# Order of the first steps of the last split in a graph-network kernel with residual normalisation

## Chip, cores and metric

One NeuronCore of a Trainium2 chip runs the whole program. The metric is the device time of one execution in microseconds (us). The engines are TensorE (PE in the profile, with PEld for its weight loads), VectorE (DVE), ScalarE (ACT), GpSimd (POOL) and SyncE (SP, which only issues transfers here).

## What is computed

The graph has 6250 nodes with 128 features and 100000 edges sorted by destination. Each edge gathers the features of its two ends and its own 128 attributes, multiplies the 384 values by W, normalises the 128 results, applies gamma, beta and relu, and its message is added to the node `src` of the edge. Each node's sum is added to its features and normalised again.

```python
msg_in = jnp.concatenate([x[row], x[col], edge_attr], axis=-1)
h = msg_in @ W + b
mu = jnp.mean(h, axis=-1, keepdims=True)
var = jnp.mean(jnp.square(h - mu), axis=-1, keepdims=True)
h = (h - mu) * jax.lax.rsqrt(var + LN_EPS) * gamma + beta
msg = jax.nn.relu(h)
out = jax.ops.segment_sum(msg, row, num_segments=x.shape[0])
...
x = _layernorm(x + out)
```

## The kernel before

The edges go through in six splits (`SPLITS`). The first half of the work on an edge computes the part of `h` that comes from the destination and the edge's own attributes, and scatters these rows to DRAM by an indirect transfer (L596), sorted by blocks of source nodes. The second half of the work loads the sorted rows back (`load_pair`, tile `hl`) and treats them by pairs of source blocks (`Pair`). Fifty blocks make 25 pairs per split; the last split has four tiles of 128 rows per pair. While the edges of one split are scattered, the pairs of the split before it are worked on (`FLOW`, `work`). After the last scatter has landed, nothing is left but the 25 pairs of the last split, and this tail is written out by hand: `head()` once and `tail(i)` for i = 0 to 24. The order of the calls is the order of the instructions on PE, DVE, ACT, SP and, in this part, POOL (`manual_schedule`).

One pair goes through these steps, which are called by these names below:

- **ones** (L668, DVE): the one-hot matrix `ohe` of the source node of each row, in one of four buffers.
- **turn** (L680, PE): four 128x128 transposes of `ohe` into a bank of PSUM, and **turned** (L684, ACT), the copy of that bank to `ohn` in SBUF, in one of two buffers.
- **seed**: the sorted rows are put into a PSUM bank (`sel` or `hp`). `seed_by_pe` (L696) does it with a product by the identity, in fp32; `seed` (L690) does it with a copy.
- **pick** (L710, PE): twelve bf16 products that add the source's features, held in three bf16 parts, to the seeded bank.
- **roots** (L1085 and L1089, ACT): four squares with sums, and the square root for the standard deviation.
- **scale** (L1145 and L735, DVE): the reciprocal, and four operations that give the messages `msg`, in one of two buffers.
- **sums** (L744, PE): four fp32 products of `ohe` and `msg`, which the profile counts as eight, into the one bank `pa`, and **add** (L762, DVE), which adds this bank to `acc`.
- For the blocks that are done, `Finish`: **load** (L774, SP) of the nodes' features `xs`, **begin** (L779 and L780, POOL), **stats** (L809, DVE), **squares** (L820, ACT) and **end** (L847, POOL). The last pair's blocks get theirs early, by `begin` and **counts** (L793, DVE).

PSUM has the banks `hp` (two), `sel` (three), `tr` (one), `pa` (one) and one for constants (`BANKS`, L35). In the tail before the change, all turns use `tr`, and pairs are seeded by PE into `sel` and `hp` in turn. Ahead of the tail PE runs some products on constants (`warm`, L1181); the last four of these wait for the last scatter. In `head()`, `work(1)` and `work(4)` are the last steps of the pair that is left over from the split before: its sums, then its add ("old sums" and "old add" below).

Of the kernel before, what the change touches and what calls it, by code (L numbers as in the profile page):

```python
# [8 lines left out]
F32 = mybir.dt.float32  # L9
BF16 = mybir.dt.bfloat16  # L10
# [6 lines left out]
P = 128  # L17
D = 128
# [9 lines left out]
PT = 4  # L28
# [6 lines left out]
BANKS = {"hp": 2, "sel": 3, "tr": 1}  # L35
# [31 lines left out]
def dram_ap(t, offset, ap):  # L67
    return bass.AP(tensor=t.tensor, offset=t.offset + offset, ap=ap)
# [12 lines left out]
def flat(t):  # L81
    return t.rearrange("p t d -> p (t d)")


def fast_path(ctx, tc, io, bad_d):
# [3 lines left out]
    nc = tc.nc  # L89
# [3 lines left out]
    psum = ctx.enter_context(tc.tile_pool(name="psum", bufs=1, space=bass.MemoryType.PSUM))  # L93
# [5 lines left out]
    def pe(i, cost=1):  # L99
        done.append((i.ins, cost))  # L100
        return i
# [69 lines left out]
    iota_p, zero_p, at = beside[:, 0:P], beside[:, P:P + 1], beside[:, P + 8:P + 8 + NB]  # L171
# [167 lines left out]
    acc = tabs.tile([P, NB, ACW], F32, name="acc")  # L339
# [306 lines left out]
    def load_pair(s, p):  # L646

        k = 2 * SPLITS[s][1]
        pair = late["blk"].tile([P, KMAX, ROW], F32, name="hl", bufs=4)
        nc.sync.dma_start(flat(pair[:, :k, :]),  # L650
                          dram_ap(sorted_d[s], p * k * P * ROW, [[k * ROW, P], [1, k * ROW]]))
        loaded[s, p] = pair

    class Pair:
# [14 lines left out]
                                    self.hl[:, :k, D:D + 1].to_broadcast([P, k, P]),  # L669
                                    row_bc(iota_p, k), op=ALU.is_equal)  # L670

        def turn(self):

            self.ohn = late["blk"].tile([P, KMAX, P], BF16, name="ohn", bufs=2)
            half = self.ohe.bitcast(BF16)
            for j0, m in [(0, self.k)]:
                tr = psum.tile([P, PT, P], F32, name="tr", bufs=BANKS["tr"]).bitcast(BF16)
                tr = tr.rearrange("p t (h d) -> p (t h) d", h=2)
                for j in range(m):
                    pe(nc.tensor.transpose(tr[:, j, :], half[:, j0 + j, 1::2], ident_h))  # L680
                self.tr = tr
# [1 line left out]
        def turned(self):  # L683
            nc.scalar.copy(self.ohn[:, :self.k, :], self.tr[:, :self.k, :])  # L684

        def seed(self, g):

            j0, m = self.groups[g]
            self.sel[g] = psum.tile([P, PT, P], F32, name="sel", bufs=BANKS["sel"])
            nc.scalar.copy(self.sel[g][:, :m, :], self.hl[:, j0:j0 + m, 0:D])  # L690

        def seed_by_pe(self, g):
            j0, m = self.groups[g]
# [182 lines left out]
    tr = psum.tile([P, PT, P], F32, name="tr", bufs=BANKS["tr"])  # L876
# [102 lines left out]
    def work(n):  # L979

        nonlocal n_steps
        for _ in range(n):
            for off, step in FLOW:
                i = n_steps - LEAD - off
                if i % 4 or not 0 <= i // 4 < len(pairs):
                    continue
                if step is None:
                    load_pair(*pairs[i // 4])
                    continue
                if off == 0:  # L990
                    at_work[i // 4] = Pair(*pairs[i // 4])
                step(at_work[i // 4])
            n_steps += 1
# [24 lines left out]
    for s, (n_tiles, _, _, _) in enumerate(SPLITS):  # L1018
        p0, p1 = first_tile[s] // PT, -(-first_tile[s + 1] // PT)
        slots = p1 - p0  # L1020
        for i in range(slots):
# [14 lines left out]
            n = steps_due(q + 1) - n_steps  # L1036
# [28 lines left out]
    s, n = n_split - 1, NB // 2  # L1065
    x = [Pair(s, p) for p in range(n)]
    f = [Finish(2 * p, 2) for p in range(n)]

    def at(p):
        return 0 <= p < n  # L1070
# [5 lines left out]
    def squares_of(i):  # L1076
        if i not in squares:
            squares[i] = late["blk"].tile([P, PT + FN], F32, name="ss6", bufs=4)
        return squares[i]

    def roots(i):
        ss = squares_of(i)
        sq = late["blk"].tile([P, PT, P], F32, name="sq")
        for j in range(PT):
            nc.scalar.activation(sq[:, j, :], x[i].sel[0][:, j, :], AF.Square, scale=float(D),  # L1085
                                 accum_out=ss[:, j:j + 1])
        c = PT + FN if at(i - 4) else PT
        std = late["blk"].tile([P, PT + FN], F32, name="std6", bufs=4)
        nc.scalar.activation(std[:, :c], ss[:, :c], AF.Sqrt, bias=eps, scale=1.0 / D ** 3)  # L1089
        x[i].std[0] = std  # L1090

    def head():
        for p in range(2):
            x[p].ones()
            load_pair(s, p + 2)
        x[0].seed_by_pe(0)
        x[0].turn()
        x[0].turned()
        f[0].load()
        work(1)  # L1100
        x[1].turn()
        x[1].turned()
        f[1].load()
        work(4)
        x[2].ones()
        load_pair(s, 4)

    both = {name: late["fin"].tile([P, 2 * FN], F32, name=name + "4", bufs=1)
            for name in ("total", "var", "std", "rstd", "shift")}
# [2 lines left out]

    def tail(i):
        x[i].pick(0)
        if i in (1, 2):
            x[i + 1].turn()
        roots(i)
        if i in (1, 2):
            x[i + 1].turned()
        if i and i + 1 < n - 1:  # L1120
            f[i + 1].load()
        if i == 0:
            f[n - 1].load()
        if i == 1:
            x[2].seed_by_pe(0)
        if at(i - 1):
            x[i - 1].sums()
        if i > 1 and at(i + 1):
            x[i + 1].seed_by_pe(0)
        if i > 1 and at(i + 2):  # L1130
            x[i + 2].turn()
        if at(i - 3) and at(i + 1):
            squares_of(i + 1)
            f[i - 3].squares(squares[i + 1][:, PT:])
        elif at(i - 3):
            f[i - 3].squares(both["var"][:, 0:FN])
        if i > 1 and at(i + 2):
            x[i + 2].turned()
        if i == n - 1:
            f[i - 2].stats()  # L1140
        if i >= n - 2:
            x[i - 1].add()
        c = PT + FN if at(i - 4) else PT
        rstd = late["blk"].tile([P, PT + FN], F32, name="rstd6", bufs=4)
        nc.vector.reciprocal(rstd[:, :c], x[i].std[0][:, :c])  # L1145
        x[i].rstd[0] = rstd
        if at(i - 4):
            f[i - 4].rstd = rstd[:, PT:]
        if 0 < i < n - 2:
            x[i - 1].add()  # L1150
        x[i].scale(0)
        if at(i + 5):
            load_pair(s, i + 5)
        if at(i - 1):
            f[i - 1].begin()
        if i == 1:
            f[n - 1].begin()
        if at(i - 2) and i < n - 1:
            f[i - 2].stats()
        if at(i - 4):  # L1160
            f[i - 4].moved()
            f[i - 4].end(nc.gpsimd, nc.sync)
        if i == 2:
            f[n - 1].counts(acc[:, 2 * n - 2:2 * n, D:D + 1])
        if at(i + 3):
            x[i + 3].ones()

    n_last = 4 * len(pairs) + LEAD + 14
# [27 lines left out]
    for i in range(n):  # L1196
        tail(i)
# [274 lines left out]
```

## Time and profile before

| quantity | value |
|---|---|
| runs shown | 1100.59, 1098.43 and 1100.34 us, median 1100.34 us |
| the profiled execution, its own time | 1102.5 us |
| its span, first to last instruction | 1100.6 us |
| mean granted clock of TensorE | 0.891 |
| busy shares | PE 78%, DVE 79%, ACT 67%, POOL 75% |
| last scatter issued | 1013.55 us, landed by 1015.62 us |
| first squares of the last split | 1023.06 us |
| last instruction that computes | 1094.4 us |

The tail that the change touches is the stretch from about 1015 us to the end. Rows of the timeline give start and length in us, engine, line, operation and tiles, the count, and in brackets the idle time of the engine ahead of it and what ended it. Rows of the chain give the start, the length and what the program's end was waiting for then. Rows by stretches give the stretch, its length, the busy time of PE with its count of products, the granted clock (1.00 is full speed), the busy share of the DMA engines and GB/s.

### The profile page before, as it was taken

The numbers are of one execution on the slowest core, as the hardware profiler recorded it, in microseconds if no ns is written. First come the engines' busy times: TensorE is split into PE (matmuls) and PEld (weight loads), VectorE is DVE, ScalarE is ACT, GpSimd is POOL, SyncE is SP. The second block draws the span as 40 slices with busy tenths as digits, with TensorE's granted clock in tenths as the row PEclk, the third lists the DMA queues.
The fourth block names the chain that finished last, engine by engine and source line by source line (L and its number), as shares of the span: only waits on it lengthen the run. The fifth ranks groups of instructions, "written<-read, shape, count | busy, mean of one in ns | idle before, by whom it ended". The sixth has DMA issues, their size and how long they took to land.

```text
span 1100.6 us, 27337 instructions
## 1 busy us (share of the span) xinstructions
PE 861.5 (78%) x8722; PEld 797.5 (72%) x8722; DVE 865.8 (79%) x2399; ACT 732.3 (67%) x3093; POOL 820.8 (75%) x907
## 2 busy tenths in 40 slices
PE   6757764638786968788877878888988899987996
PEld 4656764527776867787767778888988798885775
DVE  8875888336787877777787777988999998876897
ACT  3333331116666767576667677987989899986797
POOL 5777777777777777777777777777777777776586
PEclk8878786567898998888989898998999999999998
DMA  6999997367686865686777658876878677762563
GB/s 203 280 286 281 290 294 239 116 200 243 211 280 218 256 198 154 226 259 217 254 245 232 198 159 290 272 238 225 274 231 275 214 209 232 235 180 89 169 200 112
DMA packets 126451, 247.31 MB, mean 225 GB/s; under 512 B 47314, under 2 KB 60868, under 8 KB 126296
## 3 DMA queue, kind: packets, MB, share of 16 engines
q1 hardware_dynamic: 100118, 191.57, 57.7%
q0 software_dynamic: 25024, 52.85, 13.4%
q8 instruction: 70, 1.15, 0.5%
q10 hardware_dynamic: 1154, 1.05, 0.3%
q14 instruction: 85, 0.70, 0.2%
HBM read 155.48 MB, written 89.90 MB: 223 GB/s over the span
## 4 chain that ended last, share of the span: by engine, by line
PE 29%; DMA 28%; DVE 21%; ACT 13%; issue 5%; POOL 2%; SPq 1%; ACTq 0%; POOLq 0%; DVEq 0%
DMA sorted<-hs,place_i 20%; PE pa L744 8%; PE hp L555 7%; PE sel L710 6%; DVE msg L735 6%; DMA db<-drel_d 4%; DVE sc L412 4%; DVE ohe L668 3%; ACT sq L719 2%; POOL sorted L596 2%; PE beside L448 2%; ACT sel L690 2%; ACT sq L1085 2%; ACT ohn L684 2%; DMA eT<-in_eT 2%
## 5 line engine op out<-in xcount | busy, mean ns | idle before, releaser
L596 POOL DMA_INDIRECT sorted<-hs,place_i x782 | 760.3, 972 | 243.8 <-issue 106.0
L710 PE MATMUL sel<-xa,ohn 128*128 128x128 bf16 x2706 | 201.2, 226 | 99.2 <-ACT sel L690 98.3
L555 PE MATMUL hp<-w,eT 128*128 128x128 f32 x1564 | 244.0, 305 | 37.8 <-ACT hs L575 32.7
L575 ACT COPY hs<-hp 128x512 f32<-128x512 f32 x195 | 113.5, 582 | 240.0 <-DMA sorted<-hs,place_i 186.1
L744 PE MATMUL pa<-msg,ohe 128*128 128x130 f32 x1900 | 262.5, 290 | 11.5 <-DVE acc L762 8.2
L710 PEld LDWEIGHTS <-ohn 128*128 128x128 bf16 x2850 | 184.0, 101 | 111.6 <-issue 94.5
L735 DVE SCALAR_TENSOR_TENSOR msg<-sel,rstd,cut 128x128 f32<-128x128 f32 x902 | 255.3, 345 | 8.0
L744 PEld LDWEIGHTS pa<-msg,ohe 128*128 128x128 f32 x1900 | 238.9, 201 | 17.5 <-DVE acc L762 11.6
L555 PEld LDWEIGHTS hp<-w,eT 128*128 128x128 f32 x1564 | 218.0, 215 | 42.1 <-ACT hs L575 36.0
L719 ACT ACTIVATE sq<-sel 128x128 f32<-128x128 f32 x850 | 224.3, 282 | 17.5 <-PE sel L710 17.0
L719 ACT ACTIVATION_READ_ACCUMULATOR sq<-sel 128x1 f32 x850 | 180.4, 212 | 0.0
L668 DVE TENSOR_TENSOR ohe<-hl,beside 128x1024 f32<-128x1024 f32 (+2 forms) x150 | 148.6, 991 | 37.3 <-DMA hl<-sorted 31.5
L690 ACT COPY sel<-hl 128x512 f32<-128x512 f32 (+1 forms) x225 | 127.9, 568 | 16.3 <-DVE msg L735 16.1
L684 ACT COPY ohn<-tr 128x1024 bf16<-128x1024 bf16 (+2 forms) x150 | 123.3, 822 | 12.4 <-PE tr L680 12.2
L545 DVE TENSOR_SCALAR ohd<-db,part_w 128x512 bf16<-128x512 bf16 x192 | 70.6, 368 | 46.7 <-DMA db<-drel_d 29.8
L728 DVE RECIPROCAL rstd<-std 128x4 f32<-128x4 f32 (+1 forms) x225 | 38.5, 171 | 78.2 <-ACT std L722 77.5
L680 PE MATMUL tr<-ident_h,ohe 128*128 128x128 bf16 x950 | 81.4, 226 | 9.7 <-DVE ohe L668 9.6
L567 PE MATMUL hp<-win,ohd 126*128 126x128 bf16 x782 | 82.8, 232 | 1.3 <-DMA win<-xb_d 0.8
L680 PEld LDWEIGHTS <-ohe 128*128 128x128 bf16 x950 | 62.9, 101 | 26.1 <-DVE ohe L668 24.1
L722 ACT ACTIVATE std<-ss,eps 128x4 f32<-128x4 f32 (+1 forms) x225 | 66.9, 297 | 7.3
L567 PEld LDWEIGHTS <-ohd 126*128 126x128 bf16 x782 | 66.5, 105 | 5.8 <-DVE ohd L545 1.1
L762 DVE TENSOR_TENSOR acc<-acc,pa 128x260 f32<-128x260 f32 x124 | 51.1, 412 | 23.2 <-PE pa L744 22.4
(196 smaller groups left out, 838.4 us busy)
## 6 DMA issues: line engine op xcount, KB each, us to landing
eT<-in_eT SPq DMA_DIRECT2D x96, 512.0 KB
hl<-sorted SPq DMA_DIRECT2D x75, 528.0 KB
db<-drel_d SPq DMA_DIRECT2D x96, 256.0 KB
sorted<-empty SPq DMA_DIRECT2D x100, 198.0 KB
hl<-sorted SPq DMA_DIRECT2D x50, 264.0 KB
sorted<-hs,place_i POOLq DMA_INDIRECT x782
hl<-sorted SPq DMA_DIRECT2D x25, 396.0 KB
sorted<-empty SPq DMA_DIRECT2D x50, 132.0 KB
```

The lines of the kernel that those rows point to most:

```text
L555: pe(nc.tensor.matmul(hp[:, j, :], eT[:, at], w[:, 2, :], start=j == 0, stop=False, skip_group_check=True), 4)
L567: pe(nc.tensor.matmul(hp[:, j, :], oh[:3 * WN, at], win[:3 * WN, :], start=False, stop=j == m - 1, skip_group_check=True))
L575: nc.scalar.copy(hs[:, :m, 0:D], hp[:, :m, :])
L596: i = nc.gpsimd.indirect_dma_start(out=sorted_d[s][:, :], out_offset=bass.IndirectOffsetOnAxis(ap=place_i[:parts, t:t + 1], axis=0), in_=h ...
L668: nc.vector.tensor_tensor(self.ohe[:, :k, :], self.hl[:, :k, D:D + 1].to_broadcast([P, k, P]), row_bc(iota_p, k), op=ALU.is_equal)
L680: pe(nc.tensor.transpose(tr[:, j, :], half[:, j0 + j, 1::2], ident_h))
L684: nc.scalar.copy(self.ohn[:, :self.k, :], self.tr[:, :self.k, :])
L690: nc.scalar.copy(self.sel[g][:, :m, :], self.hl[:, j0:j0 + m, 0:D])
L710: pe(nc.tensor.matmul(sel[:, j, :], self.ohn[:, j0 + j, :], xa[:, b, i * D:(i + 1) * D], start=False, stop=j == m - 1 and i == 2, skip_gro ...
L719: nc.scalar.activation(sq[:, j, :], self.sel[g][:, j, :], AF.Square, accum_out=ss[:, j:j + 1])
L735: nc.vector.scalar_tensor_tensor(self.msg[:, j0 + j, 0:D], self.sel[g][:, j, :], rstd[:, j:j + 1], cut, op0=ALU.mult, op1=ALU.max)
L744: pe(nc.tensor.matmul(self.pa[:, h, :], self.ohe[:, j, :], self.msg[:, j, :], start=(j == h), stop=(j == k - 2 + h)), 4)
```

## The change

Only `head()`, the first four calls of `tail(i)` and two helpers change; all instructions up to the start of `head()` stand in the same order on PE. `turn` and `seed` take the name of a bank, and `seed` the engine of its copy:

```diff
-        def turn(self):
+        def turn(self, name="tr"):
...
-                tr = psum.tile([P, PT, P], F32, name="tr", bufs=BANKS["tr"]).bitcast(BF16)
+                tr = psum.tile([P, PT, P], F32, name=name, bufs=BANKS[name]).bitcast(BF16)
...
-        def seed(self, g):
+        def seed(self, g, copy=nc.scalar.copy, name="sel"):
...
-            self.sel[g] = psum.tile([P, PT, P], F32, name="sel", bufs=BANKS["sel"])
-            nc.scalar.copy(self.sel[g][:, :m, :], self.hl[:, j0:j0 + m, 0:D])
+            self.sel[g] = psum.tile([P, PT, P], F32, name=name, bufs=BANKS[name])
+            copy(self.sel[g][:, :m, :], self.hl[:, j0:j0 + m, 0:D])
```

```diff
         for p in range(2):
             x[p].ones()
             load_pair(s, p + 2)
+        f[n - 1].load()
+        work(1)
         x[0].seed_by_pe(0)
         x[0].turn()
         x[0].turned()
+        x[1].turn("hp")
+        x[1].turned()
+        x[1].seed(0, nc.vector.tensor_copy, "hp")
         f[0].load()
-        work(1)
-        x[1].turn()
-        x[1].turned()
         f[1].load()
-        work(4)
         x[2].ones()
         load_pair(s, 4)
+        work(4)
+        x[3].ones()
...
         x[i].pick(0)
-        if i in (1, 2):
-            x[i + 1].turn()
+        turns = {0: (2, "tr"), 1: (3, "sel"), 3: (4, "tr")}.get(i)
+        if turns:
+            x[turns[0]].turn(turns[1])
         roots(i)
-        if i in (1, 2):
-            x[i + 1].turned()
+        if turns:
+            x[turns[0]].turned()
         if i and i + 1 < n - 1:
             f[i + 1].load()
-        if i == 0:
-            f[n - 1].load()
-        if i == 1:
-            x[2].seed_by_pe(0)
-        if at(i - 1):
-            x[i - 1].sums()
-        if i > 1 and at(i + 1):
+        if i > 1:
+            x[i - 1 if i > 2 else 0].sums()
+        if i and at(i + 1):
             x[i + 1].seed_by_pe(0)
-        if i > 1 and at(i + 2):
+        if i == 2:
+            x[1].sums()
+        if i > 2 and at(i + 2):
             x[i + 2].turn()
...
+        if i == 2:
+            x[0].add()
+            f[0].begin()
+            x[4].ones()
...
-        if 0 < i < n - 2:
+        if 1 < i < n - 2:
             x[i - 1].add()
         x[i].scale(0)
...
-        if at(i - 1):
+        if i > 1:
             f[i - 1].begin()
-        if i == 1:
+        if i == 0:
             f[n - 1].begin()
+            f[n - 1].counts(acc[:, 2 * n - 2:2 * n, D:D + 1])
...
-        if i == 2:
-            f[n - 1].counts(acc[:, 2 * n - 2:2 * n, D:D + 1])
-        if at(i + 3):
+        if i > 1 and at(i + 3):
             x[i + 3].ones()
```

The rows below show how this moves the instructions at three places. First PE, at the start of `head()`, before the change (`pa` with `msg_2126` are the old sums; of the four transposes and their weight loads one is shown):

```order
L1192 TENSOR_LOAD bad_t
L696 MATMUL sel<-hl,ident 128x512
...
L680 MATMUL tr<-ident_h,ohe 128x128
L744 MATMUL pa<-msg_2126,ohe 128x130 x4
...
L710 MATMUL sel<-xa,ohn 128x128
...
L696 MATMUL hp<-hl,ident 128x512
...
```

And the same place with the change:

```order
L1197 TENSOR_LOAD bad_t
L744 MATMUL pa<-msg_2126,ohe 128x130 x4
L696 MATMUL sel<-hl,ident 128x512
...
L680 MATMUL tr<-ident_h,ohe 128x128
...
L680 MATMUL hp<-ident_h,ohe 128x128
...
L710 MATMUL sel<-xa,ohn 128x128
...
```

The old sums now stand ahead of the first seed, the turn of pair 1 follows that of pair 0 at once in another bank, and the seed of pair 1 (`hp<-hl`) is gone from PE.

Second ACT, from the start of `head()` on, before (the numbers at `ss` and `std` tell the pairs apart: `ss_15388` is pair 0, `ss_15428` pair 1, `ss_15481` pair 2, `ss_15537` pair 3):

```order
L684 COPY ohn<-tr 128x512 x2
L1085 ACTIVATE sq,ss_15388<-sel 128x128 x4
L1089 ACTIVATE std_15394<-ss_15388,eps 128x4
L1085 ACTIVATE sq,ss_15428<-hp 128x128 x4
L1089 ACTIVATE std_15434<-ss_15428,eps 128x4
L684 COPY ohn<-tr 128x512
L1085 ACTIVATE sq,ss_15481<-sel 128x128 x4
L1089 ACTIVATE std_15487<-ss_15481,eps 128x4
L684 COPY ohn<-tr 128x512 x2
L1085 ACTIVATE sq,ss_15537<-hp 128x128 x4
```

And with the change (pairs 0 to 3 are `ss_15400`, `ss_15440`, `ss_15473` and `ss_15536`):

```order
L684 COPY ohn<-hp 128x512
L1085 ACTIVATE sq,ss_15400<-sel 128x128 x4
L1089 ACTIVATE std_15406<-ss_15400,eps 128x4
L684 COPY ohn<-tr 128x512
L1085 ACTIVATE sq,ss_15440<-hp 128x128 x4
L1089 ACTIVATE std_15446<-ss_15440,eps 128x4
L684 COPY ohn<-sel 128x512
L1085 ACTIVATE sq,ss_15473<-sel 128x128 x4
L1089 ACTIVATE std_15479<-ss_15473,eps 128x4
L1085 ACTIVATE sq,ss_15536<-hp 128x128 x4
L1089 ACTIVATE std_15542<-ss_15536,eps 128x4
L684 COPY ohn<-tr 128x512
```

The copy for pair 2 now stands behind the root of pair 0 and that for pair 3 behind the root of pair 1, and the copy for pair 4 has moved behind the root of pair 3.

Third DVE, at the same place, as a piece of the difference (`msg_2127` is pair 0 and later pair 2, `msg_2126` pair 1):

```order
+L690 COPY hp<-hl 128x512
 L668 TENSOR_TENSOR ohe<-hl,beside 128x512
-L1145 RECIPROCAL rstd_15398<-std_15394 128x4
-L735 SCALAR_TENSOR_TENSOR msg_2127<-sel,rstd_15398,cut 128x128 x4
+L762 TENSOR_TENSOR acc<-acc,pa 128x260
 L668 TENSOR_TENSOR ohe<-hl,beside 128x512
-L1145 RECIPROCAL rstd_15446<-std_15434 128x4
-L762 TENSOR_TENSOR acc<-acc,pa 128x260
-L735 SCALAR_TENSOR_TENSOR msg_2126<-hp,rstd_15446,cut 128x128 x4
+L1151 RECIPROCAL rstd_15409<-std_15406 128x4
+L735 SCALAR_TENSOR_TENSOR msg_2127<-sel,rstd_15409,cut 128x128 x4
+L793 SCALAR_TENSOR_TENSOR last_y<-beside,acc,last_y 128x128 x2
```

DVE now copies the rows of pair 1 into `hp`, makes the one-hots of pairs 2 and 3 ahead of the first messages, and does the counts of the last blocks between the messages of pairs 0 and 1. On SP, the load of `xs` for the last blocks stands ahead of those for pairs 0 and 1, and the load of pair 5's rows follows that of pair 4's without one of `xs` in between; on POOL, `begin` of the last blocks stands ahead of that of pair 0.

More of the change, by code (lines that the diff above doesn't have):

```diff
@@ L1136, in tail @@
             f[i - 3].squares(both["var"][:, 0:FN])
-        if i > 1 and at(i + 2):
+        if i > 2 and at(i + 2):
             x[i + 2].turned()
```

## Prediction

> **What bounds the kernel now.** I read the chain of waits first, from the last scatter to the end, since only the tail changes.
>
> ```profile
> 1023.93 0.67 PE hp L710 x12
> 1024.60 0.22 PE tr L680 x4
> 1024.83 0.91 PE sel L696 x2
> ...
> 1030.57 0.95 PE pa L744 x8
> 1031.52 0.86 PE sel L696 x2
> ...
> 1033.37 1.15 ACT sq L1085 x8
> 1034.52 0.02 issue
> 1034.55 0.30 ACT std L1089
> 1034.85 0.77 ACT fsq L820 x4
> 1035.62 0.47 ACT ohn L684
> ...
> 1084.76 1.14 ACT sq L1085 x8
> ```
>
> From the landing of the first rows at 1018.39 to the squares of pair 4 at 1033.37 the chain lies on PE without a gap. From there ACT repeats squares, root, squares of the finished blocks and copy, 19 times in 1084.76 - 1033.37 = 51.39 us, or 2.70 a pair. The change leaves this steady part and the last steps as they are. So what it is worth is how much earlier the squares of pair 4 start: **1033.37** is the number to move. Second I read how PE begins, in the timeline.
>
> ```profile
> 1015.62 1.89 PE L1181 MATMUL tr<-ones_h 128*128 128x512 bf16 x4 [3.94 <-DMA sorted<-hs,place_i]
> 1018.39 2.07 PE L696 MATMUL sel<-hl,ident 128*128 128x512 f32 x2 [0.89 <-DMA hl<-sorted]
> 1020.26 0.63 PE L680 MATMUL tr<-ident_h,ohe 128*128 128x128 bf16 x4
> 1020.69 1.44 PE L744 MATMUL pa<-msg,ohe 128*128 128x130 f32 x8
> ...
> 1022.19 0.83 PE L710 MATMUL sel<-xa,ohn 128*128 128x128 bf16 x12
> ```
>
> PE stands still for 0.89 us between the products on constants and the first seed, and the seed takes 1020.26 - 1018.39 = 1.87 us, where later ones take 0.91. The granted clock says why, in stretches of 3.41 us that fit its steps:
>
> ```profile
> 106.59:110.01 3.42, 2.88 (x15) 0.50 0.93 269
> 110.01:113.42 3.41, 2.60 (x15) 0.50 0.96 338
> 669.79:673.20 3.41, 2.84 (x22) 0.50 1.04 391
> 673.20:676.61 3.41, 3.41 (x42) 1.00 1.03 358
> 1011.12:1014.53 3.41, 0.56 (x3) 1.00 0.18 60
> 1014.53:1017.94 3.41, 1.89 (x4) 0.50 0.33 91
> 1017.94:1021.36 3.42, 2.96 (x9) 0.50 0.91 298
> 1021.36:1024.77 3.41, 3.41 (x42) 1.00 0.39 127
> ```
>
> After the idle stretch from 1011.12 the clock is halved; it comes back at 1021.36, behind a stretch in which PE was busy for 2.96 us. Elsewhere 2.84 of 3.41 us busy was enough and 2.88 was not, so the border lies about there; 1.89 us did not do.
>
> **The change part by part**, first with the clock as it was here, full from 1021.36 on.
>
> *Old sums first.* They leave 1020.69 and start behind the products on constants, at 1015.62 + 1.89 = 1017.51. At full clock they take 0.95 us by the chain, so at half clock about 1.9: until 1019.4, past the landing of the rows by 1.0. The seed follows with its 1.87 to 1021.3, then the turn of pair 0 to about 1021.6, and its copy. In exchange nothing stands between the two turns any more:
>
> ```profile
> 1020.93 0.59 ACT L684 COPY ohn<-tr 128x512 bf16<-128x512 bf16 x1 [10.86 <-PE tr L680]
> ```
>
> The first copy starts at 1021.7 instead of 1020.93 and takes 0.59, so the first pick starts at 1022.3 where it was 1022.19: **0.1 us later**. The old pick had waited for the old sums and the second turn, not for its copy.
>
> *Seed of pair 1 on DVE.* PE loses one seed, **0.91 us** on the chain. DVE gains a copy of 128x512 from SBUF to PSUM, which the trace does not show. The nearest rows are ACT's copy of that size and DVE's of a quarter of it:
>
> ```profile
> 1004.88 0.58 ACT L690 COPY sel<-hl 128x512 f32<-128x512 f32 x1
> ...
> 1008.99 0.29 DVE L1186 COPY beside<-beta 128x128 f32<-128x128 f32 x1
> ```
>
> It costs between 0.29 and four times that, 1.16; I take 0.6. DVE has the two first one-hots behind it at 1019.8 and is next needed for the root of pair 0 at about 1024.6. In between lie this copy, two one-hots and the old add, by the rows further down 0.6 + 2 x 0.68 + 0.43 = 2.4 of the 4.8 us, so even 1.16 is hidden.
>
> *Turns sooner, one-hots sooner.* No turn is added; each only stands ahead of a pick or of sums where it stood behind one before, so that ACT's copy is done while PE is at other work.
>
> *Sums of pairs 0 and 1 put off to step 2.* Here new waits come in, so I walk through PE, starting with pick 0 at 1022.3 (pick 0.67, turn 0.22, seed 0.88 between the two rows of it, sums 0.95). Up to pick 2 stand two picks, two turns and a seed: 1024.95. Pick 2 needs the copy for pair 2, which ACT makes behind pair 0's squares and root: squares start 0.87 behind the pick (1022.19 and 1023.06 before), so 1023.2 + 1.16 + 0.30 + 0.5 = 1025.2: a wait of 0.25. The sums of pair 0 and the seed of pair 3 end at 1027.7. The sums of pair 1 now meet the one bank `pa`: they need the add of pair 0, which stands on DVE behind the messages of pair 1. These start at 1026.8 (copy to 1025.2, squares and root of pair 1 to 1026.65, reciprocal) and take, as do the other operations of DVE here, by the rows
>
> ```profile
> 1025.82 0.68 DVE L668 TENSOR_TENSOR ohe<-hl,beside 128x512 f32<-128x512 f32 x1
> 1026.41 0.17 DVE L1145 RECIPROCAL rstd<-std 128x4 f32<-128x4 f32 x1
> 1026.67 0.43 DVE L762 TENSOR_TENSOR acc<-acc,pa 128x260 f32<-128x260 f32 x1
> 1027.01 1.12 DVE L735 SCALAR_TENSOR_TENSOR msg<-hp,rstd,cut 128x128 f32<-128x128 f32 x4
> ```
>
> Messages and add are 1.12 + 0.43 with an overlap of 0.1: 1028.2, a wait of 0.5. Queued behind these sums are pick 3 and, through it, ACT's squares of pair 3. Pick 3 ends at 1029.8, its turn, the sums of pair 2, the seed of pair 4 follow, the turn of pair 5 waits some 0.1 for its one-hot on DVE, and pick 4 starts at 1032.2, where it was 0.87 ahead of 1033.37, or 1032.50.
>
> The **sum** in this clock: 0.1 later at pick 0; off PE go the seed's 0.91 and the waits that it had between pick 0 and pick 4, which are the 10.31 us between them less four picks, turns and seeds and three sums (9.93), or 0.38; new waits of 0.25 + 0.5 + 0.1 = 0.85 come in. That is **-0.3 us**: squares of pair 4 at 1033.1, and 1102.2 for the profiled execution's 1102.5 (its span is 1100.6). The unknown copy adds nothing between its bounds. The new waits, which I added up from rows, may come to between 0 and 1.5 us: -1.2 to +0.3.
>
> *The clock.* The steps of the granted clock lie on a grid of 3.41 us, and in this execution a boundary, 1017.94, lies just ahead of the first seed. Before the change, a stretch that holds the whole idle 0.89 has at most 2.52 us busy, less than the 2.88 that did not do, so a sufficient one begins at 1017.8 or later and full clock comes between 1021.2 and 1024.6, by where the grid lies: on average 1022.9. This execution had nearly the best case. With the old sums in the gap PE is busy from 1015.62 on; a sufficient stretch may begin at 1015.0, and full clock comes between 1018.4 and 1021.8, on average 1020.1. A product takes twice as long at half clock, so each us of it on PE's chain costs 0.5: (1022.9 - 1020.1) x 0.5 = **1.4 us** on average. That nothing fixes the grid to the program is my choice; one trace can't show it, though the runs shown, 2.16 us apart, leave room for it.
>
> The Trainium skill, "TensorE: Matmul & The Clock Gate", Part 1, says that the clock is released by a window of 4096 cycles (3413 ns) that runs freely and lies differently from run to run; the steps of 3.41 us agree, the free running no run here shows yet. The same part advises against fitting to the cold start, since it varies; by that alone the sum would be the 0.3 without the 1.4.
>
> Together 0.3 + 1.4: **-1.7 us** from the median of 1100.34, which is **1098.6**. In the profiled execution's own terms the change gives 1102.2 if the grid lies as it did, and at best, with full clock at 1018.4, half of 3.0 us less, 1100.7. The profiled time is 2.2 above the median, and I take the difference over to the median unchanged.
>
> **The rivals.**
>
> *Only the order counts* (the clock comes back where it did, as the grid goes with the program): -0.3, 1100.0. For it speaks that one grid is all I have seen; against it the spread of the runs.
>
> *The put-off sums cost nothing.* If DVE is quicker with the messages of pair 1 and the add, PE runs without the 0.85 of new waits; then -0.3 - 0.85 - 1.4, or 1097.8. ACT allows it: from pair 0's squares at 1023.2 it has four times squares and root (1.45), four copies (0.47) and 0.77 before pair 4, and so 1031.7. Against it speaks the single bank `pa`.
>
> *Slower: the counts hold DVE.* They now stand ahead of pair 1's messages and wait for POOL's `begin` of the last blocks, which needs the old add (about 1021.5) and the loaded `xs`. By the rows
>
> ```profile
> 1028.63 0.69 POOL L779 TENSOR_TENSOR last_y<-acc,g 128x256 f32<-128x256 f32 x1
> 1029.39 0.73 POOL L780 TENSOR_TENSOR last_y<-last_y,xs 128x256 f32<-128x256 f32 x1
> ```
>
> POOL's two operations end 1.49 us after they start, so they are ready by about 1023 to 1024, and the counts' turn comes at 1026. Each us that POOL ends after 1026 shifts pair 1's messages, its sums, pick 3 and the end by a us. For more than 2.2 us slower in all it would have to end at 1030. Against it speaks the transfer row: what was issued by 1021.3 had landed when the queue fell silent.
>
> ```profile
> 1023.00:1024.00 1.00, 1.00 (x8) 0.43 (x7) 0.18 (x1) 0.94 (x8) 0.00 (x0) 1.00 0.03 9
> ```
>
> Here the DMA share is 0.03. If it happened, 1103.
>
> **How the numbers follow.** Forecast 0.62 (1097.8 to 1099.4), only the order 0.18 (1099.3 to 1100.6), no new waits 0.13 (1096.8 to 1098.1), slower 0.07. A measurement of this kernel can tell about 0.2% or 2.2 us from no change, so faster means below 1098.1. That takes the third case and about a third of the first, 0.13 + 0.20 = 0.33; slower 0.05 of the last case; the rest is the same, 0.62. The range leaves out the slower case and the ends of the others: 1096.9 to 1100.5.
>
> **What would show it.** The old sums start at about 1017.5, with no idle between the constants and the seed. Full clock comes at 1021.8 or sooner after a landing at 1015.6; if later, the clock term is wrong. The sums of pair 1 wait some 0.5 for the add of pair 0; if not, the second rival. ACT's squares of pair 3 follow an idle of about 1 us, and those of pair 4 start 0.3 us sooner after the last landing (17.75 us before) if the clock comes as here, up to 1.8 sooner if it comes at the earliest. The prediction is wrong if the 2.70 a pair changes, or if counts wait.

## The result and the profile after

| | before | with the change |
|---|---|---|
| median of 22 runs each, the two kernels on one chip | 1100.46 us (1096.01 to 1104.4) | 1097.92 us (1095.55 to 1100.33) |
| ratio, 95% interval | | 0.9981, [0.9972, 0.999] |
| profiled execution, own time and span | 1102.5 and 1100.6 us | 1095.55 and 1094.0 us |
| first load of the last split's rows behind the last landing, issued | 1015.71 us | 1010.22 us |
| first squares of pair 4 | 1033.37 us | 1025.99 us |
| between these two | **17.66 us** | **15.77 us** |

The forecast was 1098.6 us, so 1.7 less; measured is 2.5 less by the medians and 2.1 by the ratio. The same change once more, in a later set of runs, gave 1099.35 us for 1099.32 and a ratio of 0.9999 [0.9986, 1.0013]. Both ratios weighted by the inverse squares of their half-widths give 0.9987, give or take 0.0008: 0.7 to 2.3 us faster. The two do not agree well, and the traces will say why executions differ so.

The spans of the two profiled executions differ by 6.6 us, but 5.49 us of that lie ahead of the tail: the last scatter was issued and landed that much earlier, where no instruction was moved on PE. So I compare the last row of the table, 1.89 us. Of this stretch, PE first (timeline of the change; start, length, engine, line, operation, count, idle time ahead):

```profile
1010.27 1.89 PE L1186 MATMUL tr<-ones_h 128*128 128x512 bf16 x8
1012.00 1.06 PE L744 MATMUL pa<-msg,ohe 128*128 128x130 f32 x8
1013.01 1.12 PE L696 MATMUL sel<-hl,ident 128*128 128x512 f32 x2
1013.97 0.39 PE L680 MATMUL tr<-ident_h,ohe 128*128 128x128 bf16 x4
1014.45 0.40 PE L680 MATMUL hp<-ident_h,ohe 128*128 128x128 bf16 x4
1015.03 0.84 PE L710 MATMUL sel<-xa,ohn 128*128 128x128 bf16 x12 [0.19 <-ACT ohn L684]
1016.25 0.40 PE L680 MATMUL tr<-ident_h,ohe 128*128 128x128 bf16 x4 [0.37 <-DVE ohe L668]
```

Constants, old sums and seed follow each other without idle time, where before there were 3.94 us of waiting for the scatter and 0.89 for the rows. That the first of these two is gone is chance (the scatter was early); that the second is gone is the change. The seed takes 1.12 us where it took 2.07: the clock was not halved at all. By stretches of 3.41 us that fit the steps of the clock in this execution (length, then busy time and count of PE, PEld, DVE, ACT, POOL, then granted clock, DMA share, GB/s):

```profile
1005.52:1008.93 3.41, 2.77 (x29) 1.97 (x26) 2.32 (x10) 2.40 (x16) 2.78 (x3) 1.00 0.18 60
1008.93:1012.34 3.41, 3.06 (x20) 2.20 (x21) 1.93 (x7) 0.73 (x5) 0.00 (x1) 1.00 0.32 84
1012.34:1015.76 3.42, 3.14 (x29) 2.02 (x27) 2.23 (x4) 1.07 (x2) 0.00 (x0) 1.00 0.92 317
```

On DVE and ACT of the same timeline stand the new copy, the counts, the add that frees `pa`, the put-off sums of pair 1, and the squares of pair 3:

```profile
1014.31 0.69 DVE L690 COPY hp<-hl 128x512 f32<-128x512 f32 x1
...
1018.75 0.60 DVE L793 SCALAR_TENSOR_TENSOR last_y<-beside,acc,last_y 128x128 f32<-128x128 f32 x2
...
1020.52 0.41 DVE L762 TENSOR_TENSOR acc<-acc,pa 128x260 f32<-128x260 f32 x1
...
1020.99 1.16 PE L744 MATMUL pa<-msg,ohe 128*128 128x130 f32 x8
...
1022.86 0.28 ACT L1085 ACTIVATE sq<-hp 128x128 f32<-128x128 f32 x1 [1.78 <-PE hp L710]
```

The copy is 0.69 us, the counts waited for nothing, and ACT stood still for 1.78 us ahead of pair 3. The add ends at 1020.93 and the sums of pair 1 begin at 1020.99, but PE was at work on the seed of pair 3 until 1020.97: in this execution it stood idle for only 0.02 us ahead of these sums, not for 0.5. The chain of waits of the change, to be read beside the one of before, stays on PE far longer, to 1055.81, but at the same pitch:

```profile
1020.12 0.86 PE hp L696 x2
1020.99 1.16 PE pa L744 x8
1022.15 0.67 PE hp L710 x12
1023.04 1.15 PE pa L744 x8
1024.20 0.86 PE sel L696 x2
1025.28 0.67 PE sel L710 x12
...
1027.98 0.67 PE hp L710 x12
...
1055.81 1.15 ACT sq L1085 x8
```

Pick to pick is 1027.98 - 1025.28 = 2.70 us, as ACT's pitch was before: PE and ACT have almost the same load per pair, and which of them the chain shows is no difference in time.

### The profile page after: what moved, and what is told of

Same layout as the page of the kernel before. It is cut to its first block, busy times and chain, and to the rows that moved or that the text cites. A ratio compares the mean times of both kernels' runs of the same rounds, so it can differ in the third digit from the quotient of the medians.

```text
span 1094.0 us, 27336 instructions
## 1 busy us (share of the span) xinstructions
PE 864.0 (79%) x8720; PEld 801.1 (73%) x8720; DVE 867.9 (79%) x2400; ACT 731.5 (67%) x3093; POOL 815.2 (75%) x907
## 4 chain that ended last, share of the span: by engine, by line
PE 31%; DMA 24%; DVE 22%; ACT 15%; issue 5%; POOL 2%; SPq 1%; ACTq 0%; POOLq 0%; DVEq 0%
DMA sorted<-hs,place_i 18%; PE pa L744 9%; PE hp L555 7%; DVE msg L735 7%; PE sel L710 6%; DVE sc L412 4%; ACT sq L719 4%; DMA db<-drel_d 4%; ACT sel L690 3%; DVE ohe L668 3%; ACT hs L575 2%; POOL sorted L596 2%; PE beside L448 2%; ACT ohn L684 2%; PE hp L567 1%
## 5 line engine op out<-in xcount | busy, mean ns | idle before, releaser
L744 PE MATMUL pa<-msg,ohe 128*128 128x130 f32 x1900 | 266.1, 293 | 11.4 <-DVE acc L762 8.2
L555 PE MATMUL hp<-w,eT 128*128 128x128 f32 x1564 | 247.4, 308 | 31.8 <-ACT hs L575 26.8
L744 PEld LDWEIGHTS pa<-msg,ohe 128*128 128x128 f32 x1900 | 242.2, 203 | 17.8 <-DVE acc L762 12.2
L555 PEld LDWEIGHTS hp<-w,eT 128*128 128x128 f32 x1564 | 221.0, 218 | 36.8 <-ACT hs L575 30.2
L680 PE MATMUL tr<-ident_h,ohe 128*128 128x128 bf16 x942 | 78.5, 222 | 10.7 <-DVE ohe L668 10.5
```

The lines of the kernel that those rows point to most:

```text
L555: pe(nc.tensor.matmul(hp[:, j, :], eT[:, at], w[:, 2, :], start=j == 0, stop=False, skip_group_check=True), 4)
L744: pe(nc.tensor.matmul(self.pa[:, h, :], self.ohe[:, j, :], self.msg[:, j, :], start=(j == h), stop=(j == k - 2 + h)), 4)
```

## Experiments

**Theory A**: most of the gain is the clock's. With the old sums between the constants and the first rows, PE has fewer stretches of 3.41 us with too little work, so the clock is not halved, or comes back sooner. **Theory B**: the clock falls and comes back as it does; only the order of the steps counts, 0.3 to 0.7 us. All times were taken against the kernel before on the same chip. A difference of under 2 us is hard to see in them, so I read each trace as well by the stretch from the issue of the first load to the squares of pair 4. The table has it for all executions. "Idle" is PE's idle time between its work on constants (or the old sums) and the first seed, "half clock" the stretch around the tail's start in which the granted clock was halved, from the issue on.

| kernel | ratio to before | idle | half clock | issue to squares of pair 4 |
|---|---|---|---|---|
| before | 1 | 0.89 | -1.18 to 5.64 | 17.66 |
| late_before | 1.0032 [1.0011, 1.0052] | 1.76 | 2.03 to 8.86 | 19.21 |
| late_order_only | 1.0042 [1.0026, 1.0058] | 1.75 | 2.19 to 9.02 | 18.85 |
| order_only | 0.9991 [0.998, 1.0001] | 1.78 | 1.74 to 8.56 | 18.84 |
| e1_old_sums_first | 0.9986 [0.9966, 1.0006] | 0.46 | 1.06 to 4.47 | 17.10 |
| e3_gap_filled | 0.9984 [0.9963, 1.0004] | 1.54 | none | 16.47 |
| late_gap_filled | 1.0026 [1.0015, 1.0036] | 0 | -3.33 to 3.50 | 16.61 |
| late_after | 1.0016 [0.9996, 1.0035] | 0 | 0.10 to 3.51 | 16.22 |
| the change | 0.9981 [0.9972, 0.999] | 0 | none | 15.77 |
| change_again | 0.9999 [0.9986, 1.0013] | 0 | none | 15.69 |
| seed_back_on_pe | 0.9994 [0.9982, 1.0005] | 0.81 | none | 16.25 |
| spare_bank_sums | 0.9979 [0.9969, 0.999] | 0 | 0.42 to 3.83 | 15.54 |
| spare_bank_again | 0.999 [0.998, 1.0001] | 1.09 | none | 15.23 |
| spare_bank_less_late | 0.9984 [0.9973, 0.9995] | 0 | 0.27 to 3.69 | 15.42 |

### The late pair and what lies between

The scatters land at other times in each execution. To make them late in both kernels, two fills of the spare buffer `empty` with its zeros on POOL hold back the last four scatters:

```diff
+    hold = []
...
+            if hold:
+                tc.add_manual_dep(i.ins, hold[0], written, reason="late")
...
+    for _ in range(2):
+        late_fill = nc.gpsimd.memset(empty, 0.0)
+        tc.add_manual_dep(late_fill.ins, last_scatter[0], written, reason="late")
+    hold.append(late_fill.ins.name)
```

`late_before` is the kernel before with it:

> The kernel before with the last four scatters held back by two fills of a spare buffer on POOL, so that in every execution PE stands idle for long and the clock drops. Both theories: 4 to 9 us slower than before, PE idle for 6 us or more ahead of the products on constants, half clock at the first seed, full clock again 5.5 to 8.9 us after the issue of the first load, yardstick 17.7 to 19.4.

and `late_after` the change with it:

> The changed kernel with the same hold. Theory A: full clock comes 2.7 to 6.1 us after the issue of the first load, yardstick 15.9 to 17.4, and the time is 1.8 us below that of late_before on average (between 0.4 and 2.1 by how the grid lies). Theory B: full clock comes 5.5 to 8.9 us after the issue as in late_before, yardstick 17.4 to 18.2, time 0.3 to 0.4 below late_before.

They came out at 1106.51 and 1104.61 us beside 1102.42 for the kernel before, 1.90 us apart, where A said 1.8 and B 0.3 to 0.4; the intervals of their ratios overlap from 1.0011 to 1.0035. The traces differ by 19.21 - 16.22 = 2.99 us. In `late_before` PE waited 2.19 us for the scatter, not the 6 or more that I expected, and in `late_after` 4.19; so the two are not matched in that. Two more kernels split this up. `late_gap_filled` is `late_before` with six products on constants for the four that wait for the scatter (`warm(6, True)`):

> The kernel before with its last scatters held back (as late_before), and two products on constants more ahead of the rows, in the gap where late_before's TensorE stood still for 1.76 us. The order of the first steps is the old one. Measured from the issue of the last split's first load to the squares of pair 4. Theory A (most of the change's gain comes from the clock, which returns sooner where no gap is left): full clock 2.7 to 6.1 us behind the issue where late_before had it 8.9 behind, 16.3 to 18.0 us for late_before's 19.21, and a median some 1.4 us below that of late_before. Theory B (only the order of the steps counts, the clock returns where it did): 19.0 to 19.5 us, and a median within 0.5 us of late_before's.

It has 16.61 us, and the clock back at 3.50: as A said, 2.6 below `late_before`. The median, 1103.68 beside 1100.75, is 2.9 above the kernel before, where `late_before` was 4.1 above: 1.2 less, in the direction of A, but within the intervals. Its clock was half for 6.83 us too, but PE had waited 5.98 us for the scatter, and the drop came 3.33 us ahead of the issue. `late_order_only` is `late_after` with the old sums back where they stood:

```diff
-        work(1)
         x[0].seed_by_pe(0)
...
         f[0].load()
+        work(1)
```

> The changed kernel with its last scatters held back (as late_after), but the old sums stand behind the first turn again, so that TensorE has nothing to do between the products on constants and the landing of the first rows; seeds, turns, and the sums of pairs 0 and 1 are as in the change. Theory A: full clock 5.5 to 8.9 us behind the issue, squares of pair 4 17.3 to 18.8 us behind it where late_after had 16.22, and a median only 0.4 to 0.8 us below late_before's. Theory B: as late_after, 16.0 to 16.5 us, and a median 1.9 us below late_before's.

It has 18.85 us and the clock back at 9.02, a median of 1105.34 (six runs) beside 1100.75; the order without the filled gap is worth 19.21 - 18.85 = 0.36 us, the filled gap 18.85 - 16.22 = 2.63, as much as with the old order (2.60). The medians of `late_order_only` and `late_after` stand 4.6 and 2.2 us above the kernel before; B had them equal. PE in `late_order_only` (in the kernels that hold or have a spare bank, lines stand up to 7 further down):

```profile
1017.90 1.04 PE L1193 MATMUL tr<-ones_h 128*128 128x512 bf16 x4 [2.21 <-DMA sorted<-hs,place_i]
1020.69 2.07 PE L699 MATMUL sel<-hl,ident 128*128 128x512 f32 x2 [1.75 <-DMA hl<-sorted]
```

and its stretches:

```profile
1013.36:1016.78 3.42, 2.02 (x12) 1.28 (x12) 1.89 (x7) 0.70 (x5) 2.75 (x3) 1.00 0.17 59
1016.78:1020.19 3.41, 1.04 (x4) 0.31 (x4) 0.00 (x0) 0.00 (x0) 0.00 (x0) 1.00 0.34 96
1020.19:1023.60 3.41, 2.91 (x9) 1.69 (x10) 2.31 (x4) 0.37 (x1) 0.00 (x0) 0.50 0.90 306
1023.60:1027.02 3.42, 3.42 (x28) 3.36 (x28) 1.36 (x3) 1.04 (x4) 1.36 (x2) 0.50 0.70 234
```

The constants run at full clock and need 1.04 us, not the 1.89 of the trace of before; so 1.75 us of idle time are left. The stretch from 1016.78 holds 1.04 us of work: the rest of it is 1.12 us of waiting for the scatter and 1.25 us of this gap. The clock is halved behind it, and 2.91 us of work in the next stretch do not bring it back. In `late_after` (the constants' row and the two behind it)

```profile
1018.78 1.73 PE L1193 MATMUL tr<-ones_h 128*128 128x512 bf16 x4 [4.19 <-DMA sorted<-hs,place_i]
...
1020.30 1.94 PE L747 MATMUL pa<-msg,ohe 128*128 128x130 f32 x8
...
1022.03 1.20 PE L699 MATMUL sel<-hl,ident 128*128 128x512 f32 x2
```

```profile
1015.56:1018.97 3.41, 0.19 (x1) 0.11 (x2) 0.00 (x0) 0.00 (x0) 1.72 (x2) 1.00 0.14 45
1018.97:1022.38 3.41, 3.41 (x13) 2.71 (x12) 0.84 (x2) 0.00 (x0) 0.00 (x0) 0.50 0.66 179
1022.38:1025.80 3.42, 2.96 (x40) 2.19 (x39) 2.76 (x5) 1.86 (x9) 0.66 (x1) 1.00 0.99 332
```

the wait for the scatter costs the clock for one stretch, but that stretch is full of work, and the clock is back 0.35 us into the seed.

### One part alone

`e1_old_sums_first` is the kernel before with `work(1)` moved ahead of the first seed and nothing else:

> The kernel before with one edit: the old sums stand ahead of the first seed, all other steps stay. The yardstick is the stretch from the issue of the first load of the last split's rows (which follows the last landing at once) to the first squares of pair 4: 17.66 us in the profile before, 15.77 in that of the change. Theory A (order and clock): where the last scatter lands late enough for the clock to have dropped, full clock comes 2.7 to 6.1 us after that issue instead of 5.5 to 8.9; the old sums cost 0.3 at half clock; yardstick 16.6 to 18.1, and the time about 1 us below before. Theory B (only the order counts, the clock comes when it did): yardstick 17.9 or more, time 0 to 0.4 above before. If the clock never dropped in the profile, both say 16.0.

1101.07 us beside 1102.42, and 17.10 us from the issue on, with the clock halved for one stretch. `e3_gap_filled` is the kernel before with `warm(6, True)`:

> The kernel before with two more products on constants behind the four that wait for the last scatter (6 instead of 4), which fill PE's 0.89 us of idle ahead of the first seed; no step of a pair moves. Theory A: with the clock dropped, full clock comes 2.7 to 6.1 us after the issue of the first load, yardstick 16.3 to 18.0, time about 1 us below before. Theory B: nothing changes but for noise, yardstick 17.6 to 19.4 with the clock dropped, time within 0.3 us of before. If the clock never dropped in the profile, both say 16.2.

1100.97 beside 1102.42, and 16.47 us: the clock was never halved here, though at full clock the six products left 1.54 us idle. PE had waited only 0.41 us for the scatter, and for a clock that never drops both theories said 16.2, so this trace does not tell them apart. The stretch with that idle time shows that the clock can be kept with 1.86 us of work:

```profile
1015.70:1019.11 3.41, 1.86 (x8) 0.68 (x6) 0.65 (x1) 0.00 (x0) 0.00 (x0) 1.00 0.71 215
```

`e1_old_sums_first` and `e3_gap_filled` each give 1.4 us in the median with the old order of the other steps, as the clock's term of the prediction, but each interval reaches past 1. The opposite is `order_only`, the change with the old sums back behind the first turn:

> The change without the one step that fills the gap: the old sums stand behind the first turn again, all else as in the change, and nothing holds the scatters back. Theory A (most of the gain is the clock's, through the filled gap): 0.3 to 0.7 us below the kernel before in the median, so a ratio of 0.9994 to 0.9997; in its profile the clock returns 5.5 us or more behind the issue of the first load if it drops at all. Theory B (the order of the other steps is what counts): as the change, a ratio of 0.998.

0.8 us below the kernel before in the median (1098.53 for 1099.32), where A wanted 0.3 to 0.7 and B 2. On the same chip `change_again` came out at 1.0, so here the order alone was 0.8 us below the change in the median, the opposite of A; the two intervals overlap widely, and the medians do not settle it. The traces point to A. The stretches of this one, and those of `spare_bank_again` below, are the best matched pair of all, since PE had waited 1.35 and 1.32 us for the scatter in them, and the steps of the clock lie 1.74 and 1.50 us behind the issue:

```profile
1011.64 1.04 PE L1186 MATMUL tr<-ones_h 128*128 128x512 bf16 x4 [1.35 <-DMA sorted<-hs,place_i]
1014.47 2.08 PE L696 MATMUL sel<-hl,ident 128*128 128x512 f32 x2 [1.78 <-DMA hl<-sorted]
```

```profile
1010.07:1013.48 3.41, 1.26 (x6) 0.31 (x4) 0.32 (x1) 0.00 (x0) 0.39 (x1) 1.00 0.22 39
1013.48:1016.89 3.41, 2.42 (x7) 1.21 (x8) 2.13 (x4) 0.00 (x0) 0.00 (x0) 0.50 0.95 310
1016.89:1020.31 3.42, 3.42 (x26) 3.36 (x26) 1.56 (x3) 1.17 (x2) 0.87 (x2) 0.50 0.85 285
```

and in `spare_bank_again`, with the old sums in the gap:

```profile
1012.96 1.04 PE L1189 MATMUL tr<-ones_h 128*128 128x512 bf16 x4 [1.32 <-DMA sorted<-hs,place_i]
1013.84 1.05 PE L747 MATMUL pa<-msg,ohe 128*128 128x130 f32 x8
1015.98 1.12 PE L696 MATMUL sel<-hl,ident 128*128 128x512 f32 x2 [1.09 <-DMA hl<-sorted]
```

```profile
1011.13:1014.55 3.42, 2.10 (x14) 1.23 (x13) 0.60 (x3) 0.00 (x0) 0.64 (x1) 1.00 0.19 44
1014.55:1017.96 3.41, 2.09 (x14) 0.98 (x12) 1.96 (x3) 0.59 (x2) 0.00 (x0) 1.00 0.94 298
1017.96:1021.37 3.41, 3.36 (x43) 2.54 (x44) 2.49 (x7) 2.93 (x16) 1.40 (x2) 1.00 0.87 313
```

With 1.26 us of work the clock is lost for two stretches, with 2.10 and 2.09 it is kept: 18.84 us and 15.23. `spare_bank_again` differs in the bank too, but that acts only behind the first squares of pair 0. These come 8.77 us behind the issue in `order_only` and 5.84 in `spare_bank_again`, so the filled gap has about 2.9 us here.

`seed_back_on_pe` is the change with `seed_by_pe` for DVE's copy:

```diff
-        x[1].seed(0, nc.vector.tensor_copy, "hp")
+        x[1].seed_by_pe(0)
```

> The change, but pair 1 is seeded by TensorE again, behind the second turn, in place of VectorE's copy of 0.69 us. Theory A (the seed's 0.91 us lie on TensorE's path): squares of pair 4 0.5 to 0.9 us later than in the change, 16.3 to 16.7 us behind the issue where the clock stays full, since part of it takes up the waits that the change has behind pick 1. Rival D (ScalarE's copies and squares of pairs 0 to 2 set the pace anyway): within 0.2 us of 15.77. In the median 0.5 to 0.9 us above the change, or none.

16.25 us at a clock that stayed full, 0.48 above the change, and from the start of pair 0's seed on 16.25 - (1016.48 - 1013.83) = 13.60 for 15.77 - (1013.01 - 1010.22) = 12.98: the seed is worth **0.6 us** of its 0.91, the rest is waiting that the change has in its place (0.19 and 0.37 us in the first fence). The rival of no difference is out by the trace; its median does not decide it, since its ratio, 0.9994, lies between the two of the change, 0.9981 and 0.9999.

### The one bank

`spare_bank_sums` is the change with the sums of pair 1 in the bank of the turns:

```diff
-            pa_t = psum.tile([P, 512], F32, name="pa")
+            if name == "pa":
+                pa_t = psum.tile([P, 512], F32, name="pa")
+            else:
+                pa_t = flat(psum.tile([P, PT, P], F32, name=name, bufs=BANKS[name]))
...
-            x[1].sums()
+            x[1].sums("tr")
```

> The change, but the put-off sums of pair 1 go to the bank of the turns, which is free then, and so wait no longer for the add of pair 0. Theory A (the one bank costs something, as the 1.78 us idle of ScalarE ahead of the squares of pair 3 suggests, which is more than the prediction's 1): these sums start without a wait, that idle time shrinks to about 1.4 us, the squares of pair 4 come 0.3 to 0.4 us sooner, 15.4 us behind the issue of the first load for 15.77 where the clock stays full. Theory C (pick 3 waits for its copy and its seed anyway): 15.7 to 15.9. In the median either is within 0.5 us of the change.

In `late_after`, with the one bank, the seed of pair 3, the sums of pair 1 and the squares of pair 3 stand so:

```profile
1028.65 1.02 PE L699 MATMUL hp<-hl,ident 128*128 128x512 f32 x2
...
1030.10 1.16 PE L747 MATMUL pa<-msg,ohe 128*128 128x130 f32 x8 [0.43 <-DVE acc L765]
...
1031.96 0.28 ACT L1088 ACTIVATE sq<-hp 128x128 f32<-128x128 f32 x1 [1.78 <-PE hp L713]
```

and in `spare_bank_sums`, whose first squares come at the same 6.15 us behind the issue:

```profile
1022.84 1.02 PE L696 MATMUL hp<-hl,ident 128*128 128x512 f32 x2
...
1023.70 1.06 PE L747 MATMUL tr<-msg,ohe 128*128 128x130 f32 x8
...
1025.46 0.28 ACT L1088 ACTIVATE sq<-hp 128x128 f32<-128x128 f32 x1 [1.09 <-PE hp L710]
```

The wait of 0.43 is gone, ACT idles 0.69 less, and the squares of pair 4 come at 15.54 for 16.22, 0.68 us sooner, twice what I expected. Where neither clock was halved it is 15.23 for 15.69, or 0.46, but there the first squares came 0.22 us later in the kernel with the spare bank. From the first squares of pair 0 to those of pair 4 it is 10.07 us in all five executions with the change's steps and one bank (`order_only` and `late_order_only` among them), at either clock, and 9.38 or 9.39 in all three with the spare bank: 0.68 us. Beside the change on one chip:

> The change itself, on the same chip as the three other kernels here, so that they can be set against it. Every theory expects a ratio to the kernel before of about 0.998; in the profile VectorE's copy takes 0.69 us, and the put-off sums of pair 1 wait for the add of pair 0 by about 0.4 us whatever the clock does.

The copy took 0.69 us again. The ratio came out at 0.9999, not 0.998, and PE stood idle for 0.08 us ahead of the put-off sums, not 0.4: as in the first profile of the change, its wait came sooner, ahead of the third turn (0.31 us).

> The change with the put-off sums of pair 1 in the bank of the turns, once more beside the change. The profile so far says 0.69 us sooner than the change at the same return of the clock (15.54 for 16.22 us), all of it between the seed of pair 3 and pick 3. If that holds in the median: 0.4 to 0.9 us below the change here. If something behind takes it back: no difference.

1097.38 us beside 1099.35, 2.0 below in the median and more than the 0.4 to 0.9 expected; the intervals, [0.998, 1.0001] and [0.9986, 1.0013], overlap. The last kernel has the spare bank, and of the four products that wait for the scatter only two:

```diff
-    warm(4, True)
+    warm(4)
+    warm(2, True)
```

> The spare bank, and of the four products on constants that wait for the last scatter only two are left; four more stand ahead, without a wait. Where TensorE waits for the scatter by some us, it idles 0.9 us less, and at half clock the old sums no longer run past the landing of the first rows by 0.5 us, as they did in the change with late scatters: squares of pair 4 14.5 to 15.6 us behind the issue. Where the scatter is early, TensorE has 0.5 us more to do, and loses up to that. Theory A: 0.1 to 0.5 us below the other kernel with the spare bank in the median; rival (the two products that are gone leave a gap at full clock, and the clock then drops or returns late): as much above it.

1097.66 us and 15.42: nothing told apart, neither a gain nor the lost clock of the rival for more than one stretch. The three runs with the spare bank have ratios of 0.9979, 0.999 and 0.9984, so this version beats the kernel before; that it beats the change, the traces show and the medians only suggest.

## Why the prediction was right, point by point

- **Old sums first: right, and more than it said.** In both profiles of the change and in `late_after` no idle time is left between constants and seed. It is not so in every execution: where the constants waited for the scatter but ran at full clock, 0.46 to 1.09 us were left behind the old sums (`e1_old_sums_first`, `seed_back_on_pe`, `spare_bank_again`). At half clock they take 1.94 us (forecast 1.9) and run past the landing of the rows by some 0.5 (forecast 1.0).
- **Seed on DVE: right.** 0.69 us for the 0.6 taken, hidden; it saves 0.6 of the 0.91, since the waits that came in took the rest.
- **New waits: the sum about right, the places not.** Pick 2 did not wait for its copy. In the change's own profile pick 0 waited 0.19 us for its copy, the third turn 0.37 for its one-hot and the sums of pair 1 only 0.02, which is 0.58 for the 0.85 forecast; in `late_after` pick 0 waited 0.46 and these sums 0.43, which is 0.89. The sign that the prediction named, some 0.5 ahead of these sums, is therefore missing in the change itself. Still the rival of no new waits does not hold: in the five executions with the change's steps and one bank the sums of pair 1 begin 5.07 or 5.08 us behind the first squares, as soon as the add of pair 0 is done, whether PE waits right there or earlier, and the spare bank takes 0.68 us off. ACT's idle time ahead of pair 3 was 1.78, not 1.
- **The order in all: right at the squares of pair 4.** -0.3 forecast; -0.36 in the late kernels with the gap open, -0.39 with it filled (16.61 and 16.22). With a clock that stayed full it is 16.47 - 15.77 = 0.70, of which the old sums in the idle time are a part. Not all of this reaches the end: from the issue to the end of the span `e3_gap_filled` takes 83.76 us and the change 83.78, and of the late kernels `late_before` takes 86.59, `late_order_only` 86.19, `late_gap_filled` 84.02 and `late_after` 83.83. There the filled gap is worth 2.4 to 2.6 us and the order 0 to 0.4.
- **The clock: the mechanism right, the size off.** The step that was off is "Before the change, a stretch that holds the whole idle 0.89 has at most 2.52 us busy", and with it the average of 2.8 us of half clock and 1.4 us. In that trace the constants had run at half clock; at full clock they leave 1.75 to 1.78 us idle, and in the three executions where they did so, this gap and the end of the wait for the scatter together took the clock away ahead of the first seed. In the four executions with the gap open the clock was half for 6.83 us; with the old sums first for 3.41 us (four executions) or not at all (four), where the prediction had it halved ahead of the tail in every case. Between the other executions set against each other above, the term is 2.6 to 2.9 us, against half of 3.0 at best in the prediction; between the profiles of before and of the change it is 1.2 to 1.5 us, the 1.89 less the 0.36 to 0.70 of the order. No execution with the gap open kept full clock, so that the term can be 0 is not shown.
- **The total: in part luck.** The 1.4 was an average over one size of gap that full clock does not leave, and over an even spread of the grid that the traces do not show (next point). The medians give 1.5 us for the whole change, give or take 0.8. From the issue to the end of the span the change takes 84.85 - 83.78 = 1.07 us less than the kernel before in their profiles, and 86.59 - 83.83 = 2.76 less in the late pair. How often either case comes up in runs without a profile, no run here shows.
- **The grid is not fixed to the program: right.** In each execution all steps of the clock, from the first to the last, lie on one grid of 3.41 us, and behind the issue of the first load a step of that grid comes by 0.09 to 2.23 us in the 14 executions. Counted from the first instruction of the span it lies at 0.63 to 3.35 us, and at 2.00 and 3.35 in the two profiles of the change, which are the same program. So the grid does not go with the program, and the reason that the rival "only the order counts" gave is out. The Trainium skill, "TensorE: Matmul & The Clock Gate", Part 1, has this window as free-running with a phase that varies from run to run; these 14 agree. Behind the issue none fell between 2.23 and 3.41, so an even spread, as I had assumed for the average, is not shown.
- **Counts: no wait.** POOL's `begin` was done by 1018.1, ahead of their turn at 1018.75. The slower rival is out.
- **The steady 2.70 us a pair: right**, but for single longer instructions, below.

## What to carry to other kernels

A short idle stretch ahead of a dependent phase costs more than itself if it lets the clock fall: look at the work in each stretch of 3.41 us on both sides of it, and move work that is there anyway into the gap. One trace shows one position of this grid and one landing time; read both as drawn by lot, and make the unlucky case on purpose before sizing the gain. Where put-off work meets a single buffer, look for a bank that is free at that time.

## What was not expected of the hardware

The share of work that keeps or brings back the clock can only roughly be bounded here. Next to the tail, stretches of 3.41 us with up to 1.26 us of PE's work lost it, and those with 1.86 and more kept it. Elsewhere in the change's profile one with 1.93 us lost it, as the stretch behind it shows, and one with 1.45 kept it:

```profile
8.82:12.24 3.42, 1.93 (x12) 1.18 (x12) 3.15 (x13) 2.84 (x7) 0.46 (x1) 1.00 0.12 29
12.24:15.65 3.41, 2.52 (x14) 1.44 (x13) 2.70 (x10) 0.74 (x2) 0.00 (x0) 0.50 0.18 39
...
285.30:288.72 3.42, 1.45 (x13) 1.27 (x13) 1.98 (x7) 1.20 (x3) 2.51 (x4) 1.00 0.82 248
288.72:292.13 3.41, 2.36 (x34) 2.35 (x34) 0.94 (x4) 3.38 (x18) 2.80 (x3) 1.00 0.31 102
```

At half clock 2.73, 2.88 and 2.91 did not bring it back, 2.84 and 2.96 did. As these overlap, busy time is not the whole rule.

In every trace but that of before, one or two instructions of DVE in the steady part are longer than their like, each time at another place, and ACT's next squares come later by as much. In the change it is the shift of one block:

```profile
1064.71 0.16 DVE L838 SCALAR_TENSOR_TENSOR shift<-total,rstd 128x2 f32<-128x2 f32 x1
...
1067.41 0.48 DVE L838 SCALAR_TENSOR_TENSOR shift<-total,rstd 128x2 f32<-128x2 f32 x1
```

From the squares of pair 4 to the end of the span are 67.23 us before and 68.01 in the change: about half of the 0.8 are two such places, the other half lies behind the last computation, which was done 5.7 and 6.1 us ahead of the end. The kernels with the old order have 67.2 to 68.1 there, those with the new one 67.3 to 68.6, so I can't tell whether the change has a part in it; the cause stays open.
